# Deformable attention, local part: dense rows of all heads in one transfer per tile, A in one per head, values by quarters in DRAM, all on SP's queue

## The chip, the cores and the metric

The program runs on one core of a Trainium2 chip, in float32. The metric is the device time of one execution in microseconds. Before the change three runs took 7682.11, 7709.34 and 7716.46 us, with a median of 7709.34. One further execution was recorded by the hardware profiler; all durations of instructions come from it.

## What is computed

The network has four layers on x (4 images of 64 x 64 positions, 128 channels). The change is in the first operator of the first layer, a deformable attention with four heads of 32 channels. Everything after it is untouched. Cut to what matters:

```python
qkv = depthwise3x3(x @ w_qkv + b_qkv) + b_dw
mask = sigmoid(conv1x1(pconv(q)))                  # 9 taps, the same for all heads
for i in range(4):                                 # heads
    off = conv1x1(pconv_i(q))                      # (dy, dx) for each of 9 taps
    dil = 2 * i + 1                                # 1, 3, 5, 7
    k_i = bilinear(k[i], p + dil * tap + off) * mask
    v_i = bilinear(v[i], p + dil * tap + off) * mask
attn = softmax(q . k_i over the 9 taps);  out = (attn . v_i) @ w_proj + b_proj;  x = x + out
```

A bilinear sample at an offset of at most one pixel is a weighted sum over a 3 x 3 neighbourhood of the tap, with "hat" weights max(0, -o), 1 - |o|, max(0, o) in y and in x. The local part computes it so; a general branch exists for larger offsets and is not taken with these inputs.

## The kernel before, in words

**Stage.** `stage_deformable` (L366) runs `deformable_project` for the four images, then one of two branches. `deformable_project` (to L607) makes q, k, v and the offsets, and stores them in DRAM: qd and kd by channel, vd as 80 columns x 84 rows x 128 channels with a border of zeros, od (offsets and masks). Per image SP's queue carries, in order, the stores of q (L529), the reload of q (qc, L548) and its shifted copies (qs, L554), the stores of k, and od (L594). The stores of v (L571) are on ACT's queue.

**Local part.** `deformable_near` (L610) takes tiles T = 0..127, 32 for each image. A tile is two image rows, 128 positions, in units of 8 columns. Four tiles are a group c, for which DVE and POOL work at once. The stages of a tile and a group, by the main loop's step T (LAG = 14):

- `products` (L713): POOL copies the tile's queries into a block layout, two instructions at L721, into one of two tiles qm.
- `product` (L738): PE multiplies them with the padded keys kpad, 64 matmuls (L750), into four PSUM tiles S of one buffer each; `copy_products` copies them to band on ACT (L760).
- `hats` (group c at T = 4c): POOL turns the offsets of the group (tile of, loaded at L686) into hat weights (L694 to L702; mk at L700 holds the masks, and L702 multiplies them in). `hat_products` multiplies the hat weights in y and x to H, 3 x 3 weights for each tap (L708, one for each head, 324 elements). H has three buffers.
- `attention` (T = 4c + 4, L762): a unit's 128 positions lie on partitions, so each partition needs its own window of band. Copies under a mask shift the rows by the bits of the column (L771, by 4, 2, 1), and a first one (L768) by the bit of the image row. Then band times H (L775), a sum over 9 (L782), and a maximum (L790 to L792).
- `spread` (T = 4c + 7, L795): the exponential on ACT (L798), the sum and its reciprocal, and the weights times H into A, 9 instructions for heads 1 to 3 (L805), t0 for head 0 (L811), and its sum into A by 12 small ones (L815 to L818).
- `write` (T = 4c + 9, L820): A goes to DRAM, in dd, one tensor for each head and each of two buffers. It takes 16 DMAs: 4 heads x 4 quarters of 32 partitions, because the image row moves the start of a row by 3 elements. The contiguous pieces are 240 to 816 B.
- `read_dense` (T + 12, L833): dd is read back as dense rows for one tile, where the row step of dd makes each position's window land in its place. It takes 4 DMAs, one for each head, of 120 to 192 KB; heads 0 and 2 on SP's queue, 1 and 3 on ACT's (L837).
- `values` and `value_block` (T + 14, L842 and L855): v comes in blocks of 4 image rows, each as 4 DMAs of 256 KB, one for each quarter of the columns (L849), seven buffers.
- `transpose` (T + 14): 12 PE transposes of the dense rows (L868), 3 copies on ACT (L870). `weigh` multiplies them with the values (L888). After four tiles `values_done` copies the result (L900), loads x (xg, L904) and adds the bias on POOL (L905); `projection` multiplies by w_proj (L911), and POOL adds (L914); `store` writes (L920).

**What sets the order.** The instruction order of each engine and queue is fixed when the program is built. The scheduler of the framework moves work ahead where its tiles are free; `block` and `behind` (L674 to L680) put the steps' work behind PE's last block. A DMA is an instruction on SP's or ACT's sequencer. It waits for what it depends on there, and all behind it waits too. In steady state POOL's built order for four tiles, with n the group of the queries, is: qm of tile 4n, the sum L914, qm of 4n+1 and 4n+2, L905, mk, the four H products of a group (they wait for DVE's release of the buffer), qm of 4n+3, and the hats of the next group. ACT's order for a tile is: the three copies of the transposes, the tile's two D reads, in some tiles the exponential, then the four copies to band.

Of the kernel before, what the change touches and what calls it, by code (L numbers as in the profile page):

```python
# [10 lines left out]
F32 = mybir.dt.float32  # L11
I32 = mybir.dt.int32
AF = mybir.ActivationFunctionType
ALU = mybir.AluOpType
# [351 lines left out]
def stage_deformable(k, x, y, w_qkv, b_qkv, w_dw, b_dw, pconv, w_offT, b_off, grid, masks, w_proj, b_proj):  # L366
# [12 lines left out]
    nc, tc = k.nc, k.tc  # L379
    with ExitStack() as octx:  # L380
# [6 lines left out]
        far = deformable_project(k, fp, x, qd, kd, vd, od, w_qkv, b_qkv, w_dw, b_dw, pconv, w_offT, b_off)  # L387
        with tc.If(far > 0) as branch:
            deformable_general(k, x, y, w_qkv, b_qkv, w_dw, b_dw, pconv, w_offT, b_off, grid, w_proj, b_proj)
        with branch.Else():  # L390
            deformable_near(k, dr, x, y, qd, kd, vd, od, masks, w_proj, b_proj)


def deformable_project(k, fp, x, qd, kd, vd, od, w_qkv, b_qkv, w_dw, b_dw, pconv, w_offT, b_off):
# [7 lines left out]
    nc, tc = k.nc, k.tc  # L402
    HP = 66
    with ExitStack() as ctx:
# [129 lines left out]
        for b in range(4):  # L534
# [57 lines left out]
            for i in range(4):  # L592
                r, h = divmod(i, 2)
                nc.sync.dma_start(od[b][64 * h + 32 * r : 64 * h + 32 * r + 32], off[32 * i : 32 * i + 32])  # L594

# [13 lines left out]
def deformable_near(k, dr, x, y, qd, kd, vd, od, masks, w_proj, b_proj):  # L609
# [23 lines left out]
    PP = [12 * (15 + w) for w in W]  # L633
    with ExitStack() as ctx:
# [14 lines left out]
        for t in qms:  # L649
            nc.gpsimd.memset(t, 0.0)  # L650

# [5 lines left out]

        dd = [[dr.tile([128, 4 * PP[g] + 12], F32, tag=f"dd{i}{g}", name=f"dd{i}{g}") for g in range(4)] for i in range(2)]

        dense = [wp.tile([128, 4, 384], F32, tag=f"D{i}", name=f"D{i}") for i in range(4)]  # L660
        for t in dense:
            nc.gpsimd.memset(t, 0.0)
        for i in range(2):
            for g in range(4):
                zero = dense[g].rearrange("p t n -> p (t n)")
                eng = (nc.sync, nc.scalar)[g % 2]
                eng.dma_start(dd[i][g][:, 0 : 4 * PP[g]], zero[:, 0 : 4 * PP[g]])
                eng.dma_start(dd[i][g][:, 4 * PP[g] : 4 * PP[g] + 12], zero[:, 0:12])

        Hs, bands, outs, vblocks, logits, ofs, hat_of, queries = {}, {}, {}, {}, {}, {}, {}, {}  # L670
        accs, lefts, project, stores = {}, {}, [], []
# [16 lines left out]
        def hats(c):  # L688
# [10 lines left out]
            mk = sm.tile([128, 3, 4, 3], F32, tag="mk", name="mk")  # L699
            nc.gpsimd.tensor_copy(mk, window(of, 72, [[3, 3], [81, 4], [1, 3]]))  # L700
            hy = hat[:, 0:4].rearrange("p s a t n i -> p s (a t n) i")
            nc.gpsimd.tensor_tensor(hy, hy, window(mk, 0, [[0, 4], [1, 36], [0, 3]]), op=ALU.mult)  # L702
            Hs[c] = sm.tile([128, 4, 36, 9], F32, tag="H", name="H", bufs=3)

        def hat_products(c, groups):
            H, hat = Hs[c], hat_of[c]
            for g in groups:
                nc.gpsimd.tensor_tensor(  # L708
                    H[:, g].rearrange("p n (a c) -> p n a c", a=3), window(hat, 108 * g, [[3, 36], [1, 3], [0, 3]]),
                    window(hat, 108 * (4 + g), [[3, 36], [0, 3], [1, 3]]), op=ALU.mult,  # L710
                )
# [50 lines left out]
        def attention(c):  # L762
            H, band = Hs[c], bands.pop(c)
            prod = sm.tile([128, 4, 36, 9], F32, tag="prod", name="prod", bufs=1)
            for g in range(4):
                rows = lambda off, dims: window(band[g], off, [[4 * CW[g], 12]] + dims)
                n = 3 * CW[g]
                nc.vector.copy_predicated(rows(0, [[1, n]]), bit[:, 0, :, 3:4].to_broadcast([128, 12, n]), rows(CW[g], [[1, n]]))  # L768
                for i, s in enumerate((4, 2, 1)):
                    n = W[g] + s - 1  # L770
                    nc.vector.copy_predicated(  # L771
                        rows(0, [[CW[g], 3], [1, n]]), bit[:, :, :, i : i + 1].to_broadcast([128, 12, 3, n]), rows(s, [[CW[g], 3], [1, n]])
                    )
                for tx in range(3):
                    nc.vector.tensor_tensor(  # L775
                        window(prod, 324 * g + 9 * tx, [[27, 12], [3, 3], [1, 3]]),
                        window(band[g], DIL[g] * tx, [[4 * CW[g], 12], [CW[g], 3], [1, 3]]),
                        window(H, 324 * g + 9 * tx, [[27, 12], [3, 3], [1, 3]]), op=ALU.mult,
# [16 lines left out]
        def spread(c):  # L795
# [7 lines left out]
            for g in range(1, 4):  # L803
                for ty in range(3):
                    nc.vector.tensor_tensor(  # L805
                        window(A[g], ty, [[12 * DIL[g], 12], [3, 3], [12, 3]]), window(H, 324 * g + 108 * ty, [[9, 12], [3, 3], [1, 3]]),
                        window(lg, 36 * g + 12 * ty, [[1, 12], [0, 3], [0, 3]]), op=ALU.mult,
                    )

            t0 = sm.tile([128, 36, 9], F32, tag="t0", name="t0", bufs=1)  # L810
            nc.vector.tensor_tensor(t0, H[:, 0], window(lg, 0, [[1, 36], [0, 9]]), op=ALU.mult)  # L811
            for ty in range(3):
                a0 = lambda m0, n: window(A[0], 12 * m0 + ty, [[60, 4], [12, n], [3, 3]])
                tap = lambda tx, s0, n: window(t0, 108 * ty + 9 * tx + s0, [[27, 4], [1, n], [3, 3]])
# [5 lines left out]
        def write(c):  # L820
            A = As[c % 2]
            for g in (1, 2, 3, 0):
                d, P = dd[c % 2][g], PP[g]
                for j in range(4):
                    r = j % 2
                    nc.sync.dma_start(
                        bass.AP(
                            d.tensor, d.offset + 32 * j * (4 * P + 12) + 3 * r, [[4 * P + 12, 32], [P, 4], [1, 12 * W[g]]]
                        ),
# [1777 lines left out]
```

## Time and profile before

| What | Value |
|---|---|
| median of three runs | 7709.34 us (7682.11 to 7716.46) |
| the profiled execution | 7690.3 us; its span 7688.3 us |
| projection, 0 to 675 us | PE busy 566 us, DVE 126, ACT 209, POOL 11; DMA share 0.44, 105 GB/s |
| local part, 675 to 1830 us | PE busy 839 us, DVE 732, ACT 373, POOL 466; DMA share 0.71, 203 GB/s |
| granted TensorE clock | 0.94 in the first of these, 0.82 in the second |
| value blocks, vb<-vd | 272 DMAs of 256 KB |
| dense rows, D<-dd | 512 DMAs of 120 to 192 KB, half on SP, half on ACT |
| A, dd<-A | 512 DMAs of 30 to 102 KB for each head and group |

A line of the timeline has the start in us, the length, the engine, the line of the kernel, the operation, its output and inputs and their shapes; an "x4" merges four neighbours, and what stands in brackets is the engine's idle time before it and what ended it. SPq and ACTq are the DMA issues of these sequencers. A line of waits has who waited, for what, the total, the number of times and the longest. The granted clock is a share of full speed. A DMA share is the mean busy share of the 16 DMA engines.

### The profile page before, as it was taken

The page shows a single profiled execution, that of the slowest core. Times are in us where ns is not written, and L with a number is a line of the kernel's source. Part 1 is how long each engine was busy: PE and PEld are TensorE (multiplying, and loading weights), DVE is VectorE, ACT ScalarE, POOL GpSimd, SP SyncE. Part 2 cuts the span into 40 slices and gives each one's busy share as a digit, 9 for nine tenths or more (in the row PEclk, how much of TensorE's full clock was granted, in tenths as well). Part 3 has the DMA queues.
Part 4 walks back from the last instruction along what each step waited for, and adds up shares of the span by engine and source line. Part 5 has one row for each costly group of instructions (what it writes and reads, how often), then busy time and mean ns, then how long its engine had stood idle before and what let it go on. Part 6 is the DMA issues. An engine that isn't in the chain of part 4 may idle for free. (4 is left out here: it accounts for less than half of the span.)

```text
span 7688.3 us, 157708 instructions
## 1 busy us (share of the span) xinstructions
PE 6522.7 (85%) x63791; PEld 3542.4 (46%) x63791; DVE 4821.5 (63%) x11178; ACT 2690.3 (35%) x6141; POOL 1741.4 (23%) x1634
## 2 busy tenths in 40 slices
PE   7995777775688868989989999798898997997989
PEld 3343666663455644345555555445225234242244
DVE  2113766764277554858856656674785875867877
ACT  3331333333234313611146555565104013031056
POOL 0003444320001100035532221154012112120135
PEclk9997887887799889999999988798897997988989
DMA  4436677775400022030100000001111111111101
GB/s 121 98 87 179 187 209 205 213 199 172 143 4 1 2 60 48 10 117 22 27 12 10 9 10 6 9 1 30 39 25 49 26 33 40 25 35 38 25 23 31
DMA packets 678781, 495.59 MB, mean 64 GB/s; under 512 B 302326, under 2 KB 594104, under 8 KB 674200
## 3 DMA queue, kind: packets, MB, share of 16 engines
q1 hardware_dynamic: 480910, 354.59, 17.0%
q10 hardware_dynamic: 197130, 130.77, 6.2%
q8 instruction: 509, 8.34, 0.5%
q14 instruction: 232, 1.90, 0.1%
HBM read 335.28 MB, written 149.75 MB: 63 GB/s over the span
## 5 line engine op out<-in xcount | busy, mean ns | idle before, releaser
L2476 DVE TENSOR_TENSOR t<-S,q 128x1536 f32<-128x1536 f32 (+3 forms) x608 | 1156.9, 1948 | 123.2 <-PE S L2464 117.9
L2464 PE MATMUL S<-R,L 32*128 32x512 f32 x4096 | 734.6, 651 | 90.3 <-DMA R<-wd 78.9
L2492 PE MATMUL acc<-t,sum 128*32 128x512 f32 x4096 | 639.5, 608 | 0.0
L750 PE MATMUL S<-kpad,qm 32*64 32x240 f32 (+3 forms) x8192 | 403.4, 421 | 216.0 <-ACT band L760 97.5
L2178 PE MATMUL pe<-ew,yT 128*128 128x512 f32 x1024 | 479.4, 603 | 27.4 <-DVE xs L2184 24.5
L1777 PE MATMUL acc<-w,attT 128*64 128x264 f32 x4096 | 486.3, 391 | 10.4 <-DVE w L1773 10.4
L2464 PEld LDWEIGHTS S<-R,L 32*128 32x128 f32 x4096 | 200.6, 186 | 611.4 <-issue 280.4
L2498 ACT COPY agg<-acc 128x512 f32<-128x512 f32 x32 | 18.8, 586 | 1194.0 <-DMA L<-pd 626.7
L750 PEld LDWEIGHTS S<-kpad,qm 32*64 32x64 f32 x8192 | 299.9, 156 | 271.5 <-issue 136.9
L1770 POOL TENSOR_TENSOR w<-xtl,ei 128x528 f32<-128x528 f32 x256 | 332.1, 1319 | 309.6 <-ACT ei L1769 204.5
L2184 DVE SCALAR_TENSOR_TENSOR xs<-pe,gate,xs 128x128 f32<-128x128 f32 x1024 | 332.5, 345 | 96.5 <-PE pe L2178 79.8
L1773 DVE TENSOR_TENSOR w<-xtl,pe 128x1056 f32<-128x1056 f32 x256 | 320.3, 1251 | 100.3 <-ACT ei L1769 89.4
L1777 PEld LDWEIGHTS acc<-w,attT 128*64 128x64 f32 x4096 | 284.0, 137 | 197.5 <-DVE w L1774 38.0
L2187 ACT ACTIVATE sc<-pe,gate 128x128 f32<-128x128 f32 x1024 | 291.3, 374 | 202.2 <-PE pe L2178 194.1
L514 PE MATMUL dw<-pad,diag 32*32 32x512 f32 x6912 | 310.4, 614 | 12.9 <-issue 7.0
L2507 POOL TENSOR_TENSOR o<-o,bf 128x512 f32<-128x512 f32 x32 | 40.7, 1271 | 1229.4 <-ACT o L2506 1229.4
L760 ACT COPY band<-S 128x144 f32<-128x144 f32 (+3 forms) x512 | 136.0, 351 | 480.4 <-DMA D<-dd 152.3
L2492 PEld LDWEIGHTS acc<-t,sum 128*32 128x32 f32 x4096 | 92.7, 108 | 458.4 <-issue 436.1
L2178 PEld LDWEIGHTS pe<-ew,yT 128*128 128x128 f32 x1024 | 185.6, 193 | 234.3 <-issue 151.4
L768 DVE COPY_PREDICATED band<-bit,band 128x432 f32<-128x432 int32 (+3 forms) x128 | 107.5, 895 | 270.0 <-ACT band L760 264.2
L868 PE MATMUL pt<-ident,D 128*128 128x128 f32 x1536 | 243.0, 315 | 29.2 <-DMA D<-dd 15.2
L771 DVE COPY_PREDICATED band<-bit,band 128x288 f32<-128x288 int32 (+11 forms) x384 | 243.0, 742 | 0.0
(520 smaller groups left out, 13065.8 us busy)
## 6 DMA issues: line engine op xcount, KB each, us to landing
vb<-vd SPq DMA_DIRECT2D x272, 256.0 KB
D<-dd ACTq DMA_DIRECT2D x128, 192.0 KB
D<-dd SPq DMA_DIRECT2D x128, 168.0 KB
D<-dd ACTq DMA_DIRECT2D x128, 144.0 KB
w<-in_e_weight_dram ACTq DMA_DIRECT2D x16, 1024.0 KB
w<-in_e_weight_dram SPq DMA_DIRECT2D x16, 1024.0 KB
wd<-s SPq DMA_DIRECT2D x32, 512.0 KB
D<-dd SPq DMA_DIRECT2D x128, 120.0 KB
```

The lines of the kernel that those rows point to most:

```text
L514: nc.tensor.matmul(acc[g][32 * c : 32 * c + 32], diag[r, j, tap, :], pads[j][r, y0 : y0 + 8, tx : tx + 64], start=(tap == 0), stop=(tap == 8),
L750: ins = nc.tensor.matmul(acc[g][64 * h : 64 * h + 64].rearrange("p (a s) c -> p a s c", a=3), qm[rows, h, m, :], keys, start=(m == 0), sto ...
L771: nc.vector.copy_predicated(rows(0, [[CW[g], 3], [1, n]]), bit[:, :, :, i : i + 1].to_broadcast([128, 12, 3, n]), rows(s, [[CW[g], 3], [1, ...
L1770: nc.gpsimd.tensor_tensor(w2[:, 2:4], xt[:, 2:4, 0:2], window(ei, 0, [[0, 2], [0, 2], [1, 132]]), op=ALU.mult)
L1773: nc.vector.tensor_tensor(w1, xt[:, :, 1:3], window(pe, 0, [[0, 4], [0, 2], [1, 132]]), op=ALU.mult)
L1777: nc.tensor.matmul(acc[b // 2][64 * (b % 2) : 64 * (b % 2) + 64], attT[:, b // 2, hp, 64 * (b % 2) : 64 * (b % 2) + 64], src[:, b].rearran ...
L2178: nc.tensor.matmul(pe[h].rearrange("p e c -> p (e c)"), yT[:, 128 * t : 128 * t + 128], ew[:, 4 * h : 4 * h + 4, :].rearrange("p e c -> p ...
L2184: nc.vector.scalar_tensor_tensor(xt, pe[0][:, e, :], gate[:, t, e : e + 1], xt, op0=ALU.mult, op1=ALU.add)
L2187: nc.scalar.activation(sc[:, e, j, :], pe[1][:, e, :], AF.Copy, scale=gate[:, t, 4 + e : 5 + e])
L2464: nc.tensor.matmul(S[:, j, :], Ls[n % 2][r, ag, :], Rs[n % 2][r, ag].rearrange("p x y -> p (x y)"), start=True, stop=True)
L2476: nc.vector.tensor_tensor(t[:, j0:j1].rearrange("p u (x y) -> p u x y", x=8), S[:, j0:j1].rearrange("p u (x y) -> p u x y", x=8), qf[:, q0 ...
L2492: nc.tensor.matmul(acc[0][32 * h : 32 * h + 32, :], sum4, t[:, j, :], start=(u < 4), stop=(u >= 60))
```

## The change

It has six parts. In the projection, each image's padded values are copied from vd to a new tensor vq in DRAM, four overlapping quarters of 32 columns side by side, by four DMAs on SP's queue. In the local part a value block is then one DMA of 1 MB with 8 KB rows. The dense rows of all heads lie in one tensor dd for each buffer, 384 elements a head, and come in one DMA a tile (768 KB, 6 KB rows) on SP's queue, zeros with them. A goes out in one DMA a head. For that the shift by the image row moves out of the address and out of band into the weights: H has 4 x 3 weights for each tap where it had 3 x 3, and `hats` builds the four y weights from the three, the masks and the row bit; L768 goes, the shifts of band and the products with H and A cover a fourth row, and the quarters of `write` go. H has two buffers where it had three, dt three for four. xg is loaded at the first tile of its group, four tiles before. The zeros for dd come from one tile, in ten DMAs on ACT's queue. ACT issues no D reads any more.

In the built program the steady order on POOL for four tiles is: qm of 4n, mk and the sum L914, the row-bit products of mk, L905, qm of 4n+1 and 4n+2, two H products, half of the qm of 4n+3, a third H product, the other half, the fourth, and the hats of the next group. On SP's queue, one of an image's four copies to vq stands ahead of od, and three behind it.

```diff
+        vq = [dr.tile([32, 84, 4, 128], F32, tag=f"vq{b}", name=f"vq{b}") for b in range(4)]
...
             for i in range(4):
                 r, h = divmod(i, 2)
                 nc.sync.dma_start(od[b][64 * h + 32 * r : 64 * h + 32 * r + 32], off[32 * i : 32 * i + 32])
+            for q in range(4):
+                nc.sync.dma_start(vq[b][:, :, q, :], vd[b][16 * q : 16 * q + 32])
...
+    ROW = 4 * 4 * 384 + 12
+        nc.vector.tensor_copy(row, bit[:, 0, 0, 3:4])
-        dd = [[dr.tile([128, 4 * PP[g] + 12], F32, tag=f"dd{i}{g}", name=f"dd{i}{g}") for g in range(4)] for i in range(2)]
+        dd = [dr.tile([128, ROW], F32, tag=f"dd{i}", name=f"dd{i}") for i in range(2)]
-        for t in dense:
-            nc.gpsimd.memset(t, 0.0)
...
+        nc.gpsimd.memset(dense[0], 0.0)
+        zero = dense[0].rearrange("p g n -> p (g n)")
+        for d in dd:
+            for t in range(4):
+                nc.scalar.dma_start(d[:, 1536 * t : 1536 * t + 1536], zero)
+            nc.scalar.dma_start(d[:, 6144:ROW], zero[:, 0:12])
...
-            nc.gpsimd.tensor_copy(mk, window(of, 72, [[3, 3], [81, 4], [1, 3]]))
+            nc.gpsimd.tensor_copy(mk[:, 0].rearrange("p (a t n) -> p a t n", a=3, t=4), window(of, 72, [[3, 3], [81, 4], [1, 3]]))
+            nc.gpsimd.tensor_scalar(mk[:, 1], mk[:, 0], row, None, op0=ALU.mult)
+            nc.gpsimd.tensor_tensor(mk[:, 0], mk[:, 0], mk[:, 1], op=ALU.subtract)
             hy = hat[:, 0:4].rearrange("p s a t n i -> p s (a t n) i")
-            nc.gpsimd.tensor_tensor(hy, hy, window(mk, 0, [[0, 4], [1, 36], [0, 3]]), op=ALU.mult)
-            Hs[c] = sm.tile([128, 4, 36, 9], F32, tag="H", name="H", bufs=3)
+            h4 = hy_of[c] = sm.tile([128, 4, 36, 4], F32, tag="hy", name="hy", bufs=1)
+            nc.gpsimd.tensor_tensor(h4[:, :, :, 0:3], hy, at(0), op=ALU.mult)
+            nc.gpsimd.tensor_tensor(hy, hy, at(1), op=ALU.mult)
+            nc.gpsimd.tensor_tensor(h4[:, :, :, 1:3], h4[:, :, :, 1:3], hy[:, :, :, 0:2], op=ALU.add)
+            nc.gpsimd.tensor_copy(h4[:, :, :, 3], hy[:, :, :, 2])
+            Hs[c] = sm.tile([128, 4, 36, 12], F32, tag="H", name="H")
...
-                nc.vector.copy_predicated(rows(0, [[1, n]]), bit[:, 0, :, 3:4].to_broadcast([128, 12, n]), rows(CW[g], [[1, n]]))
                 for i, s in enumerate((4, 2, 1)):
                     n = W[g] + s - 1
-                    nc.vector.copy_predicated(
-                        rows(0, [[CW[g], 3], [1, n]]), bit[:, :, :, i : i + 1].to_broadcast([128, 12, 3, n]), rows(s, [[CW[g], 3], [1, n]])
-                    )
+                    nc.vector.copy_predicated(flat[:, :, 0:n], bit[:, 0, :, i : i + 1].to_broadcast([128, 48, n]), flat[:, :, s : s + n])
...
         def write(c):
-            for g in (1, 2, 3, 0):
-                d, P = dd[c % 2][g], PP[g]
-                for j in range(4):
-                    r = j % 2
...
+            for g, d in enumerate(DIL):
+                m = dd[c % 2]
+                nc.sync.dma_start(
+                    bass.AP(m.tensor, m.offset + 384 * g + 12 * (7 - d), [[ROW, 128], [1536, 4], [1, 12 * W[g]]]),
+                    As[c % 2][g][:, :, 0 : W[g]].rearrange("p t c s a -> p t (c s a)"),
+                )
         def read_dense(T):
             c, t = divmod(T, 4)
-            for g, d in enumerate(DIL):
-                m, P = dd[c % 2][g], PP[g]
-                (nc.sync, nc.scalar)[g % 2].dma_start(
...
+            m = dd[c % 2]
+            nc.sync.dma_start(
+                dense[t].rearrange("p g n -> p (g n)"), bass.AP(m.tensor, m.offset + 1536 * t, [[16 * ROW, 8], [ROW - 12, 16], [1, 1536]])
+            )
         def value_block(n):
-            for q in range(4):
-                nc.sync.dma_start(
-                    t[:, q].rearrange("p s c -> p (s c)"),
-                    bass.AP(d.tensor, d.offset + 16 * q * 10752 + 4 * kb * 128, [[10752, 32], [128, 4], [1, 512]]),
-                )
+            nc.sync.dma_start(
+                t.rearrange("p s q c -> p (s q c)"), bass.AP(d.tensor, d.offset + 4 * kb * 512, [[84 * 512, 32], [512, 4], [1, 2048]])
+            )
         def values(T):
             if T % 4 == 0:
+                inputs[0] = sm.tile([128, 4, 128], F32, tag="xg", name="xg")
+                nc.sync.dma_start(inputs[0], tokens(x, b, i, 4))
...
-                dt = sm.tile([128, 4, 128], F32, tag="dt", name="dt", bufs=4)
+                dt = sm.tile([128, 4, 128], F32, tag="dt", name="dt", bufs=3)
...
-                xg = sm.tile([128, 4, 128], F32, tag="xg", name="xg")
-                nc.sync.dma_start(xg, tokens(x, b, 4 * c, 4))
+                xg = inputs[0]
```

The products with H and A in `attention` and `spread` change their shapes from 3 x 3 to 4 x 3 and are not shown.

## The prediction

> **What bounds the kernel now.** Only the deformable stage is edited. In the table of stretches it fills the first 1830 of 7688.3 us: the projection to about 667 us, the local part from 671 to 1830. I first looked at three groups of four tiles in the middle of the local part (columns: the stretch and its length, busy PE, weight loads, DVE, ACT, POOL with instruction counts, the granted clock, the DMA share, GB/s):
>
> ```profile
> core 0: us, PE busy (x) PEld busy (x) DVE busy (x) ACT busy (x) POOL busy (x), PEclk, DMA share, GB/s
> 1412.85:1445.93 33.08, 24.18 (x694) 20.39 (x695) 23.07 (x58) 11.43 (x32) 12.05 (x20) 0.91 0.74 209
> 1445.93:1479.39 33.46, 24.34 (x700) 20.29 (x698) 23.20 (x57) 11.42 (x32) 12.42 (x20) 0.94 0.77 217
> ```
>
> No engine is full: a group takes 33 us, PE and DVE work 23 to 24 of them, the DMA engines three quarters. So a chain of waits sets the period. The view of waits over 660 to 1830 us names its links (who waited for what: total us, times, longest):
>
> ```profile
> POOL xg L905 <- DMA xg<-in_x_dram: 411.1, 24, 24.8
> ...
> ACT band L760 <- DMA D<-dd: 152.3, 29, 8.3
> ...
> PE S L750 <- ACT band L760: 97.5, 48, 6.1
> PE S L750 <- POOL qm L721: 94.0, 22, 16.6
> DVE m L799 <- ACT lg L798: 90.0, 32, 6.8
> ...
> ACT lg L798 <- DMA D<-dd: 82.6, 11, 9.4
> ```
>
> ACT, only a third busy, is held up by its own queue: it issues two of a tile's four reads of dd (L837), and while such an issue waits, the copies and the exponential behind it wait too. The timeline of one group shows where that hurts:
>
> ```profile
> 1427.44 0.31 DVE L792 TENSOR_TENSOR lg<-lg,me 128x144 f32<-128x144 f32 x1
> 1428.35 0.32 ACT L798 ACTIVATE lg<-lg 128x144 f32<-128x144 f32 x1 [6.19 <-DMA D<-dd]
> ...
> 1433.20 3.15 POOL L708 TENSOR_TENSOR H<-hat 128x324 f32<-128x324 f32 x4 [1.59 <-DVE t L811]
> ...
> 1436.30 0.45 POOL L721 COPY qm<-q 128x64 f32<-128x64 f32 x2
> ...
> 1437.55 2.20 PE L750 MATMUL S<-kpad,qm 32*64 32x144 f32 x64
> ...
> 1444.35 1.22 ACTq L837 DMA_DIRECT2D D<-dd  x2
> 1445.61 1.07 ACT L760 COPY band<-S 128x144 f32<-128x144 f32 x4 [7.24 <-DMA D<-dd]
> 1445.93 1.33 DVE L768 COPY_PREDICATED band<-bit,band 128x432 f32<-128x432 int32 x2 [8.74 <-ACT band L760]
> ```
>
> This is a closed loop, once per group. DVE's attention (1445.93 to 1460.92, 15.0 us) ends in the exponential on ACT; DVE's spread reads H until L811 (done at 1433.12); then POOL may overwrite an H buffer (L708); behind that in POOL's order stands the query copy qm; it releases PE's product of the group's last tile; its copy (L760) lets the next attention start. The product ended at 1439.75 and its copy began at 1445.61: 5.9 us behind a DMA issue. SP's own rows in these three groups (1412.85 to 1514.23) sum to 79.8 of 101.4 us of issuing: 16 writes, 8 reads and about 8 value transfers a group, each some 0.4 to 0.65 us and more beside ACT's. That is why the rows that ACT waits for land late. The exponential starts at 732.8 the first time and 1772.0 the last, so 31 periods of 33.5 us.
>
> **The change in the loop, per group.** Working against one period:
>
> - DMA issues. Reads of dd fall from 16 to 4, writes from 16 to 4, value transfers from about 8.5 to 2.1; q, x, store, offsets and keys (about 5.5) stay. SP goes from about 38 issues to 16; even at 0.7 us that is 11 us where 26 stand now. ACT issues none. The 5.9 us ahead of the copy become its usual 0.1; of the exponential's wait (90.0/32 = 2.8 us) about 0.4 stays, as at 758.74, where nothing stood in front.
> - DVE attention. The row select goes (L768: 107.5 us / 32 = 3.4). The three shifts cover 48 rows, not 36: L771 is 243.0 / 32 = 7.6 now; its rows run in steps of four elements (5, 6 and 8 wide take 527, 480 and 502 ns; 9, 10, 12 take 665, 676, 655), so about 1 ns an element on a third more, +1.9. L775 goes from 108 to 144 elements, 12 x 0.038 = +0.45; L782 from 1296 to 1728, +0.45. Net -0.5: 14.5 us.
> - DVE spread, from L799 to the end of L811: 4.4 now, +0.35 for nine products a third larger, +0.1 for L811; L805 took 2.92 us in this group because POOL's L905 ran beside it, 1.93 at 784.68 where none did, and L905 moves away. I take 4.5.
> - POOL. H grows from 324 to 432 elements. L702 does 432 in 1.0 us, so a product costs 1.05 for 0.79. In the changed order three of the four, not four, precede the whole qm copy: 3.2 + 0.45 = 3.65, for 3.6 now. H has two buffers for three, so POOL makes H one group less ahead; in both orders the qm of a group's last tile stands behind the same spread, so this adds no link.
> - PE's product with its start 3.3 (2.2 to 2.9 by clock) and the first copy 0.35.
>
> Sum: 14.5 + 0.8 (exponential with its handoffs) + 4.5 + 3.65 + 3.3 + 0.35 = 27.1 us.
>
> **What the loop then collides with.** Behind H, POOL does the next hats: today 1.4 + 1.15 + 0.7 + 0.6 + 1.0 (L694 to L702), now also a second 432 product, a 288 sum and a 144 copy: 7.0 us, ahead of the query copy of the next tile. From one qm to the next that is 8.6 us, then three unhindered steps of PE (5.0 us from 1201.96 to 1206.98) and a projection of 2: 25.9. PE alone needs 4 x 5.1 + 2 = 22.5, DVE 23.1 as now. The DMA engines: 7.67 MB a group (D is 768 KB a tile for 624, writes 1.08 MB, values 2.2 MB, the rest 1.0). At the near rows' 282 GB/s (the ACT queue moved 5.65 MB between 1100 and 1240 in 14.3% of 16 x 140 us) 27 us, at the 380 of the weight loads' rows of about 2 KB (2070 to 2080) 20. D and values, 5.4 MB in rows of 6 and 8 KB, are nearer to the second, the rest stays at 250: 23.5. All four limits stand within 5 us of the loop.
>
> The attention will also start while POOL is still in its hats, which today end before it (hats to 1441.66, attention from 1445.93). Row: at 706.96, with POOL full, the attention took 21.2 us to L792 for 15.0, so +0.4 us for each us beside POOL; against nothing, if the overlap misses the sharing instructions. About 5 us overlap, +1.7 (0 to 4). I take the period as 27.1 + 1.7 = 28.8. **Gain: 31 x (33.5 - 28.8) = 146 us.**
>
> On this point the Trainium skill speaks against the change: "SBUF — State Buffer", section "Who interferes with whom", says a DVE instruction with two SBUF inputs and a GpSimd instruction that reads SBUF share a port pair, and the second blocks entirely. By that rule the whole 5 us would be lost, a period of about 32 and a gain near 45 us; the row of 706.96 shows a partial loss only, and decides here.
>
> The skill's "DMA: Bandwidth & Descriptors", section "Issuing engines are not separate DMA queues", says that several issuing engines save only the time of issue, usually small. By it the ACT queue's end would be worth 8 x 0.6 = 4.8 us a group at most; the trace shows an issue that waits, 5.9 us on one copy alone, and that is what the sum counts.
>
> **What it costs outside the loop.** The new copies vd to vq: 16 transfers, 2688 pieces of 512 B each (1.38 MB). No row moves DRAM to DRAM. At least one read, by the 512 B rows of the x reload (290 GB/s from 1840 to 1860): 4.7 us; at most read and write in turn, the write by the ACT queue between 50 and 600 us (9.44 MB in 7.0% of 16 x 550 us, 245 GB/s): 10.4. So 19 to 42 us a batch, 14 to 31 for the three behind od. From od to the next store of q there are 49, 49 and 29 us (224.5 to 273.5, 378.2 to 427.1, 531.5 to 560.1): hidden, and if not, it adds to PE's wait for qc (22.6 us in 4). I take +3. After the last batch the cover is gone: od ends at 663.6, the first keys are issued at 678.1, and PE waits 19.5 us for them. Keys and queries stand behind three copies in SP's queue: 678 to 695, so +0 to +25; one memset of dense for four (5.3 us) gives POOL some back, but ten zero issues on ACT come before its first copies. I take +12. At the drain, PE waits 9.4 us for D at 1790; half of it goes: -5.
>
> **Sum:** 7690.3 (span 7688.3 and 2.0 around it) - 146 + 12 + 3 - 5 = 7554. The median of the runs is 7709.3, 19 us above that execution; less the same 136 it is 7573. I say 7560.
>
> **Rivals.**
> 1. The sharing costs nothing and the loop settles at 26.5 (PE and DVE's work with handoffs). For: L816's 0.77 beside H falls after L811, off the loop. Against: 7 us of hats. 31 x 7 - 12 = 205 less: 7485. Chance 0.17.
> 2. DVE and POOL block each other in attention and hats, or the one queue runs full: period 31.3. For: 706.96, and 85% of DMA time on one queue. 31 x 2.2 - 25 = 43 less: 7650. Chance 0.12.
> 3. Slower: the vq copies. One ring takes SP's transfers in turn; if a batch's copies last D us, the delays over four batches are about 4D less the gaps 49 + 49 + 29 + 15 = 142. That equals the gain in the loop, 146, at D = 72 us, 77 GB/s, beyond my upper bound by a factor 1.7; at D = 85 the time is 7690 - 146 - 5 + 198 = 7737. For: no row of such a copy; against: 512 B rows in both directions run above 240 GB/s. Chance 0.07.
> 4. The change does not remove the wait: SP in order holds read_dense behind write, write waits for the spread, and the transposes wait for D in place of ACT. Against: the next read needs no row of that write and has two steps, some 13 us, to land. Period 33: 7700. Chance 0.04.
>
> My forecast has 0.60, between 7500 and 7630. The range takes in most of rivals 1 and 2: 7470 to 7670. A change under 0.5% (38 us) cannot be told from none here: faster 0.86, same 0.06, slower 0.08.
>
> **What would show it.** No ACT issue of D, and the wait of the band copies for D gone; the exponential 0.4 us after L792; POOL's 411 us for xg gone; attention near 15 us but 1 to 3 longer where hats run beside it; exponentials 28 to 29 us apart; the first product of the local part at 685 to 710. Wrong if the attention reaches 18 us, if PE waits for D, or if the projection grows by more than 10 us.

## The result, and the profile after

The changed kernel takes 8144.1 us (median of 4 runs, 8142.0 to 8167.6), the kernel before 7696.8 us beside it (4 runs): a ratio of 1.059, 95% interval 1.055 to 1.062. The forecast was 7560 us, faster. The profiled execution has a span of 8142.0 us for 7688.3, 453.7 us more. In the local part the first exponential comes at 762.7 us (732.8 before) and the last at 2212.1 (1772.0). So 31 periods of 46.75 us stand where there were 31 of 33.5, which makes 410 us; 30 us come ahead of the first exponential, 14 behind the last. The period went the wrong way.

First the two groups of the changed kernel that answer to those shown of before (same columns: stretch and length, busy PE, weight loads, DVE, ACT, POOL, clock, DMA share, GB/s):

```profile
1414.81:1466.65 51.84, 29.21 (x860) 25.36 (x858) 20.33 (x53) 14.40 (x35) 15.32 (x25) 0.73 0.74 152
1466.65:1514.60 47.95, 20.70 (x626) 17.05 (x620) 21.43 (x53) 10.47 (x28) 12.49 (x21) 0.68 0.69 149
```

The engines do about as much work in a group as before (PE 49.9 us in these two groups for 48.5, DVE 41.8 for 46.3), the rest of the time they stand. The DMA share is the same 0.7, but it moves 150 GB/s where it moved 209 to 217. The granted clock is lower too (0.73 and 0.68 for 0.91 and 0.94), but that is not the loss: the product that stands in the loop took 2.2 us in both kernels in the median (table below). The view of waits, 760 to 2260 us, all engines and then SP's own:

```profile
DVE band L782 <- ACT band L773: 701.7, 28, 37.9
...
PE S L763 <- POOL qm L734: 487.2, 36, 30.1
POOL mk L707 <- DMA of<-od: 438.9, 21, 24.5
POOL xg L906 <- DMA xg<-in_x_dram: 435.1, 29, 33.8
```

```profile
SPq L832 <- DMA D<-dd: 495.8, 35, 22.8
SPq L921 <- POOL mk L708: 207.8, 12, 18.7
SPq L921 <- POOL xg L915: 172.4, 13, 19.9
```

ACT's waits for D are gone, as forecast. In their place POOL waits for two small loads (offsets of, and x), 28 us a group together; PE waits for POOL's query copies, DVE for PE's products. One group in the timeline shows how it goes round:

```profile
1414.81 2.39 SPq L832 DMA_DIRECT2D dd<-A  x4
...
1418.59 0.59 SPq L840 DMA_DIRECT2D D<-dd  x1
...
1420.09 1.00 SPq L691 DMA_DIRECT2D of<-od  x1
...
1438.20 0.22 POOL L707 COPY mk<-of 128x36 f32<-128x36 f32 x1 [24.51 <-DMA of<-od]
...
1438.38 1.26 POOL L915 TENSOR_TENSOR xg<-xg,o 128x512 f32<-128x512 f32 x1
...
1439.67 0.37 SPq L921 DMA_DIRECT2D x<-xg  x1
...
1441.96 0.38 SPq L862 DMA_DIRECT2D xg<-in_x_dram  x1
...
1451.16 1.26 POOL L906 TENSOR_TENSOR xg<-xg,bpj 128x512 f32<-128x512 f32 x1 [10.66 <-DMA xg<-in_x_dram]
1452.36 0.76 POOL L734 COPY qm<-q 128x64 f32<-128x64 f32 x4
...
1452.65 4.11 PE L763 MATMUL S<-kpad,qm 32*64 32x144 f32 x64 [14.91 <-POOL qm L734]
```

The offsets are issued at 1420.09 and POOL has them at 1438.20, 18 us later: in the same queue stand writes, a dense read and a value block. Meanwhile SP stands in the store (1439.67), which waits for POOL's addition (1438.38), which stands behind mk. So xg is issued only at 1441.96, POOL waits for that too, and the queries come last. PE's product, after 14.9 us of standing, takes 4.11 us here for the usual 2.2.

The links of the loop, from the starts and ends of these instructions, as medians over the 7th to 28th group (us; the rows are the prediction's; the experiments e10 to e17 are told below):

```
                                 before  after   e1    e10   e12*   e11*  e17*
exponential to last read of H      4.8    4.4    4.4   4.5    4.4    4.5   4.5
from there to H written (POOL)     3.3   17.3    7.8   3.8    3.2    4.2   3.8
to the product's start             2.8    7.1    8.0   6.0    1.4    4.1   0.8
product                            2.2    2.2    2.3   2.2    2.2    2.2   2.2
its end to DVE's attention         3.4    0.4    0.4   0.4    2.5    0.4   0.5
attention, to the exponential     17.3   17.0   16.4  16.4   17.0   17.6  19.1
period, mean of all 31            33.5   46.8   39.5  33.9   30.3   32.9  30.6
(* dense reads cut short; a median of each row need not add up to the mean)
```

The prediction's gain is there in one row, 3.4 to 0.4. Two rows, POOL's H and the way from it to the product, take 18 us back.

**The DMA engines.** A packet is one contiguous piece of a transfer, as the profile records it. From the records of single packets, 1200 to 1600 us (own sums over all sizes that occur more than 60 times, by the trace's own clock, 11 us ahead of that of the views):

```
                             before   after     e1      e8
a write of 816 B, ns           50      121      92      52
256 B loads, ns                19       32      20      21
D packets, B: ns         960 to 1536:  6144:   6144:   6144:
                          53 to 79      387     430     416
all packets, us of 400 x 16   4643     4577    5352    4999
```

In the kernel before, ACT's queue carries nothing but dense reads there, and each transfer leaves small completion packets of 4 B: 736 with the 11776 rows of 92 reads (by the clock of the views), 8.0 for each. The source of a dense read has 8 in its outermost dimension, 16 x 8 rows in all. Read as one completion packet for each engine that takes part, a dense read lay on 8 of the 16 engines; the changed kernel's has the same 8 outermost, and e3 below counts 8.0 for it too. The mean share hides that. Of the changed kernel's 4577 us, 1583 are dense packets: 1583/8 + 2994/16 = 385 of 400 us on these 8, 96%. For the kernel before the same sum gives 1606/8 + 3037/16 = 391 of 400, 98%. The records don't name the engine of a packet, so these two sums take the other packets as even over all 16.

The Trainium skill, "DMA: Bandwidth & Descriptors", section "Rules for kernel authors", states this: an outermost dimension of fewer than 16 confines a transfer to at most that many engines. The 8.0 packets agree; the page was not weighed in the prediction.

### The profile page after: what moved, and what is told of

Same layout as the page of the kernel before. It is cut to its first block, busy times and chain, and to the rows that moved or that the text cites. A ratio compares the mean times of both kernels' runs of the same rounds, so it can differ in the third digit from the quotient of the medians.

```text
span 8142.0 us, 156307 instructions
## 1 busy us (share of the span) xinstructions
PE 6531.4 (80%) x63791; PEld 3555.1 (44%) x63791; DVE 4781.7 (59%) x11051; ACT 2707.9 (33%) x6141; POOL 1798.3 (22%) x1791
## 5 line engine op out<-in xcount | busy, mean ns | idle before, releaser
L763 PE MATMUL S<-kpad,qm 32*64 32x288 f32 (+3 forms) x8192 | 388.1, 432 | 600.8 <-POOL qm L734 504.6
L782 DVE COPY_PREDICATED band<-bit,band 128x384 f32<-128x384 int32 (+11 forms) x384 | 318.1, 938 | 752.6 <-ACT band L773 701.7
L872 ACT COPY dt<-pt 128x512 f32<-128x512 f32 x384 | 209.6, 592 | 307.9 <-PE pt L870 306.0
L870 PE MATMUL pt<-ident,D 128*128 128x128 f32 x1536 | 263.8, 335 | 36.9 <-issue 21.0
```

Of the source, the lines that this page charges most:

```text
L763: ins = nc.tensor.matmul(acc[g][64 * h : 64 * h + 64].rearrange("p (a s) c -> p a s c", a=3), qm[rows, h, m, :], keys, start=(m == 0), sto ...
L782: nc.vector.copy_predicated(flat[:, :, 0:n], bit[:, 0, :, i : i + 1].to_broadcast([128, 48, n]), flat[:, :, s : s + n])
```

## Experiments

Three theories stood at the start. **A**: the 8 engines that carry the dense reads set the period. **B**: the one queue on SP does, through what stands behind what. **C**: the layout of values, with its copies and its large packets. D, E and F were formed on the way. Times are medians; those of the kernel before lay between 7682 and 7693 us beside them.

**e1: the changed kernel, dense reads over 16 engines.**

```diff
-bass.AP(m.tensor, m.offset + 1536 * t, [[16 * ROW, 8], [ROW - 12, 16], [1, 1536]])
+bass.AP(m.tensor, m.offset + 1536 * t, [[ROW - 12, 16], [16 * ROW, 8], [1, 1536]])
...
-nc.scalar.copy(dt, pt)
+nc.scalar.copy(dt.rearrange("p g (b x) -> p g b x", b=8), pt.rearrange("p g (x b) -> p g b x", b=8))
```

> The changed kernel, with the 128 rows of a dense read taken in another order: the outermost dimension of the source has 16 steps in place of 8, and the copy of the transposed tile puts the order back. Bytes, packets, queue and number of transfers stay. Theory A (a dense read lies on 8 of the 16 DMA engines; these 8 are 96% busy in the changed kernel and set the period of a group at 47.5 us): with 16 engines the sum of all packets, 2268 us in a stretch of 200 us, is 539 us a group and 34 us on each engine, less where packets get shorter with fewer in flight; period 28 to 35 us, time 7550 to 7730 us. Theory B (one queue on SP: writes of dd wait for reads of D, and everything behind them is late): a read lands some 2 us earlier, period 44 to 47 us, time 8030 to 8140 us. Theory C (packets of 6 and 8 KB move fewer bytes in a us than those of 1 and 2 KB): period 40 to 47 us, time 7900 to 8140 us.

7920.4 us, 39.5 us a group. The stretch from 1200 to 1600 us, of the changed kernel and then of e1:

```profile
1200.00:1600.00 400.00, 204.40 (x5489) 171.26 (x5473) 164.94 (x424) 97.46 (x248) 120.26 (x195) 0.71 0.71 153
```

```profile
1200.00:1600.00 400.00, 263.39 (x6726) 219.21 (x6718) 224.89 (x513) 120.65 (x304) 164.88 (x247) 0.75 0.84 187
```

A is right in kind: 7.2 of the 13.2 us a group go, and the share rises from 0.71 to 0.84. It isn't all; 39.5 lies outside its range. The time alone would also lie in C's range; e4 tests C.

**e2: the kernel before, the same order in its four reads.**

```diff
-bass.AP(m.tensor, m.offset + t * P, [[16 * (4 * P + 12), 8], [4 * P, 16], [1, P]])
+bass.AP(m.tensor, m.offset + t * P, [[4 * P, 16], [16 * (4 * P + 12), 8], [1, P]])
```

> The kernel before, with the same order of 16 in its four dense reads a tile and in the copy. Theory A: the low 8 engines were 98% busy there too (566 us of dense packets over 8 engines and 1073 us of others over 16 make 138 of 140 us), so the period of 33.5 us was theirs; with 1639 us over 16 engines (102 of 140 us) the next limit takes over at 27 to 31 us, time 7490 to 7620 us. Rival (the prediction's loop of engines with ACT's issues in it sets 33.5 us whatever the DMA engines do): 7660 to 7720 us.

7653.4 us, ratio 0.9955 (0.9938 to 0.9971), 32.2 us a group, 16.0 completion packets a read for 8.0. Between the two: the 8 engines cost the kernel before 1.3 us a group. Its 98% was not a bound: with half of the dense load taken off these 8 only 4% of the period went. Spread over 16, packets of 1536 B took 86 ns for 79, so a packet's time holds waiting too, and such sums overstate the work.

**e3: the changed kernel, dense reads of odd tiles on ACT.**

```diff
-nc.sync.dma_start(
+(nc.sync, nc.scalar)[T % 2].dma_start(
```

> The changed kernel with the dense reads of odd tiles issued by ACT, those of even tiles by SP. Theory A: every read still lies on the same 8 engines; period 46 to 48 us, time 8090 to 8180 us. Theory B (the one queue): half of the reads no longer stand ahead of SP's writes and loads; period 34 to 42 us, time 7700 to 7980 us.

8035.4 us, 42.4 us a group, between both ranges, with 8.0 completion packets a read: 4.3 us a group come from the second queue alone, with 8 engines as before. So the 96% of the changed kernel was no bound either. The run does not part what stands behind a large read in the queue from what SP, in order, issues late.

**e4: the changed kernel with the value blocks of before** (from vd, four transfers; no copies to vq).

> The changed kernel with the value blocks of before: no copies to vq, four transfers a block, packets of 2 KB. Theory A: the same bytes lie on all 16 engines; packets of 2 KB took 107 ns before, 4 of them 428 ns, against 591 ns of one of 8 KB in the changed kernel, so 2 blocks a group cost up to 2.6 us less on each engine, and the copies of the start (15 us) go: period 44 to 47.5 us, time 8010 to 8130 us. Theory C (the large value packets or the copies are the loss): period 33 to 38 us, time 7690 to 7850 us.

8100.4 us, 45.8 us a group, and the first exponential 9.5 us earlier: as A had it. C is worth 1.0 us a group.

**e5: e1 with three buffers of dd** (`range(3)`, `c % 3`).

> Run e1 (changed kernel, reads of D over 16 engines: 39.5 us a group, 7920 us) with three buffers of dd in memory in place of two, so that a write of dd no longer waits for reads of two groups earlier (305.8 us of SP's waits in e1, 9.5 us a group). Theory B (SP's one queue stands still behind that wait, and all its other loads come late): period 31 to 35 us, 7680 to 7800 us. Theory A, as e1 left it (the work of the DMA engines: sum of all packets 33.4 us a group on each of 16 engines, 85% of the time; what waits in SP's queue would only wait in the engines): period 37 to 39.5 us, 7850 to 7930 us.

7891.6 us, 38.35. The wait of SP's writes for D left the list; in its place the writes waited 250 us for DVE's A (44.5 in e1), and SP's store waited 370 us for POOL, as long as in e1 (366 us). B in this form falls: the queue stands as before, behind other waits.

**e6: e1 with e3's edit.**

> Run e1 with the reads of D of odd tiles issued by ACT. In the changed kernel itself the same edit took 109 us off (46.75 to 42.4 us a group). Theory B: SP is relieved of half of the large reads, period 33 to 36 us, 7720 to 7810 us. Theory A as e1 left it: the engines' 33.4 us a group stay, period 37 to 39.5 us, 7850 to 7930 us.

7806.8 us, 36.15, the time at the upper end of B's range, the period just above it: a second queue is worth 3.4 us a group on 16 engines too.

**e7: e1 with four dense reads a tile, of the used columns only.**

```diff
+for g, d in enumerate(DIL):
+    o, n = 12 * (7 - d), 12 * (15 + W[g])
+    nc.sync.dma_start(
+        dense[t][:, g, o : o + n],
+        bass.AP(m.tensor, m.offset + 1536 * t + 384 * g + o, [[ROW - 12, 16], [16 * ROW, 8], [1, n]]),
+    )
```

> Run e1 with each dense read in four, one a head, of the columns that the head uses (as in the kernel before: 624 KB a tile for 768, packets of 960 to 1536 B for 6144), all on SP. Theory A as e1 left it (bytes and packet times): a tile's 128 rows cost 128 x (0.053 + 0.069 + 0.068 + 0.079) = 34 us of engine time by the packets of before in place of 128 x 0.43 = 55 us, 5.2 us a group on each engine; period 33 to 36 us, 7720 to 7830 us. Theory B (waits in SP's queue): SP issues 12 more transfers a group and still waits; period 38 to 42 us, 7880 to 8010 us.

7847.9 us, 37.8, neither range: 1.8 us a group for 19% fewer dense bytes, a third of the 5.2 that A had. Packets of 960 and 1536 B took 80 and 102 ns here, not the 53 and 79 of before.

**e8: e1 with rows of dd 512 B longer** (`ROW = 4 * 4 * 384 + 12 + 128`).

> Run e1 with rows of dd 512 B longer, so that the rows that 16 engines read at once lie 25088 B apart and not 24576 B (6 x 4096). Theory D (rows at multiples of 4 KB hit the same part of the memory, so that a packet of 6144 B takes 430 ns in e1 for 234 ns where one read runs alone): packets of 300 ns or less, 4 us a group less on each engine, period 34 to 36 us, 7750 to 7830 us. Theories A and B: no change, 39 to 40 us, 7900 to 7940 us.

7857.6 us, 37.4. The time fits neither range. The theory had the wrong object: the dense packets hardly changed (430 to 416 ns), but the writes of 816 B fell from 92 to 52 ns, the time of before, and the value packets of 8 KB from 525 to 420. That the longer rows do this is measured; which of the two the 2.1 us a group come from, and why, is not known. The writes have a row step of 24624 B and the reads one of 24576, and the edit lengthens both.

**e9: e1 with all dense reads on ACT.**

> Run e1 with all reads of D issued by ACT, so that SP's queue holds no large read. Theory B (small loads and writes of SP land late because they stand behind D in one queue): beyond e6 (half of the reads on ACT: 36.15 us a group, 7807 us) a further gain, 33 to 35.5 us, 7700 to 7790 us. Theory A (16 engines' work, 84 to 87% busy in e1 and e6): 36 to 37 us, 7800 to 7840 us. Rival (ACT's copies wait behind its issues, as in the kernel before): 37 to 41 us, 7840 to 7960 us.

7855.0 us, 37.7, worse than half of them on ACT. The time lies in the rival's range, but ACT's waits show no D among the larger ones, so the rival isn't shown. SP's waits don't explain it either: its store waited 355.2 us for POOL's addition (101.1 in e6), but the load of xg behind it waited less for the store to land, 99.1 us for 324.2, and so did the writes for D, 231.7 us for 339.8. Why e9 is slower than e6 stays open.

**e10: all that helped, together** (e6, e8's rows, e5's buffers, e4's values).

> All that helped, together: the changed kernel with reads of D over 16 engines, odd tiles' reads on ACT, rows of dd 512 B longer, three buffers of dd, and the value blocks of before without the copies to vq. If the parts add up (from e6's 36.15 us a group: the stride 2.1 by e8, the third buffer 1.2 by e5, the values 1.0 and 10 us at the start by e4): 31.9 us a group, 7630 to 7720 us. If they share one wait: 33.5 to 35.5 us, 7720 to 7790 us.

7728.6 us, ratio 1.0041 (1.0027 to 1.0054), 33.9 us: the parts do not add up to 31.9; time and period lie in the range of parts that share one wait. 416 of the 447 us are back, and the changed kernel is still not the faster one.

**e11: the changed kernel with dense reads of 96 columns for 1536** (three more memsets at the start).

> The changed kernel with dense reads cut to 96 of 1536 columns (the output lacks the rest of the local attention); every instruction, wait and transfer stays, only the bytes of D go. Prediction's loop of engines (28.8 us, and 28 to 30 us between the first exponentials of the changed kernel, before any dense read): 28 to 30.5 us a group, 7560 to 7640 us. Theory B in its strong form (order in SP's queue and not bytes): 36 us or more, over 7800 us.

7690.1 us, 32.9, neither. The bytes of D cost 13.8 of 46.75 us. What stays is 4.1 us over the 28.8 of the prediction's loop. Two of e11's waits, from 760 to 1850 us:

```profile
PE S L764 <- POOL qm L735: 193.7, 46, 10.7
...
POOL H L722 <- DVE t L821: 166.7, 28, 11.9
```

**e12: the kernel before with dense reads of 24 columns a head.**

> The kernel before with its four dense reads a tile cut to 24 columns each (the output lacks the rest of the local attention); all instructions and waits stay. If its loop of engines is the one seen between its first exponentials, before any dense read (24.6 to 25.5 us): 25 to 28 us a group, 7430 to 7530 us: then the change made the loop 4 us longer and the kernel before was held back by its reads. If ACT's waiting issues set 33.5 us as the prediction had it, whatever the bytes: 31 to 33.5 us, 7610 to 7700 us.

7589.2 us, 30.3, neither. Here D's bytes cost 3.3 us. So **without the bytes the change makes the loop 2.7 us longer** (30.3 to 32.9), where the prediction had it 4.7 us shorter. The two waits of e11 are 31.8 and 53.5 us here. The second, POOL's wait for an H buffer, points at a rival that no run tries: H with two buffers for three (and dt with three for four).

**e13, e14, e15: offsets two steps earlier, the store one step later** (in e11, in e10, and in e2, there with xg loaded early as well).

```diff
-step(T, -2, offsets, 4)
+step(T, -4, offsets, 4)
...
-late = list(stores)
+late = [s for s in stores if T >= s[3] + 2]
```

> Run e11 (changed kernel, reads of D cut to 96 columns: 32.9 us a group, 7690 us) with the load of the offsets two tile steps earlier and the store of the result one step later (the output still lacks the rest of the local attention). In e11 SP stands 301.6 us (10 us a group) in the store behind POOL's addition of the result, POOL then stands behind the load of the offsets that SP issues later. Theory E (SP and POOL, each in order, wait for each other in turn, and this makes 32.9 of the 28.8 that the prediction had): 29 to 31 us, 7570 to 7640 us. Rival F (POOL's own work, 19 us a group for 14 in the kernel before, and its stretches beside DVE): 32 to 33.5 us, 7660 to 7710 us.

> Run e10 (changed kernel with 16 engines, two queues, wider rows, a third dd, values as before: 33.9 us a group, 7729 us) with the same two moves. Theory E: 30.5 to 32.5 us, 7620 to 7690 us. Rival F or the DMA engines (88% busy in e10): 33 to 34.5 us, 7700 to 7740 us.

> Run e2 (kernel before with reads of D over 16 engines: 32.2 us a group, 7653 us) with the same two moves and with xg loaded at the first tile of its group, as in the changed kernel. POOL's waits for xg (278.8 us and 124.7 us, 12 us a group in e2) go. If they are on the path: 29 to 31 us, 7530 to 7610 us; if not: 32 to 33 us, 7630 to 7680 us.

7687.7, 7726.4 and 7651.1 us: no change from e11, e10 and e2. That is as rival F had it, but it does not refute E, because the moves did not take the waits away. From the first exponential to the last, SP's store waited 280.9 us for POOL's addition in e13 (282.6 in e11) and 145.8 in e14 (128.0 in e10), and POOL waited 408.9 us ahead of adding to xg in e15 (371.1 in e2). So E stays open, and in the changed kernel itself it wasn't tried.

**e16: e14 with the query copies on ACT.**

```diff
-nc.gpsimd.tensor_copy(
+nc.scalar.copy(
     window(qm, 256 * h, [[32, 2], [72, 4], [1, 8]]),
```

> Run e14 with the copies of the queries (qm) on ACT in place of POOL. In e11 a copy of 36 elements on POOL that began in DVE's attention took 5.28 us in place of 0.3, in the kernel before a qm copy up to 8.8 us in place of 0.24, and the products wait for qm. Theory F (POOL is held up beside DVE and its order carries qm): 1.5 to 3 us a group less than e14, 50 to 90 us. Rival (ACT, in order, then brings qm behind its copies of products): same as e14 or up to 60 us slower.

7707.2 us (7698.3 to 7729.5), some 19 us less than e14 (7712.6 to 7749.4). That is a smaller gain than F's and not the rival's loss; the DMA share is 0.90, so another limit may stand near.

**e17: the same edit in e11. e18: in e2.**

> Run e11 (changed kernel with reads of D cut to 96 columns, output without the rest of the local attention) with the copies of the queries on ACT: e16 made the same edit where the DMA engines were 90% busy, here they are at 53%. In e11 a POOL copy that began at 1389.36 in DVE's attention lasted 5.28 us, to 0.06 us after the attention's last product, and the query copies behind it came at 1396.63. Theory F (POOL and DVE hold each other up in the attention, and POOL's order carries the queries): the product no longer waits for POOL, 29 to 31.5 us a group, 7580 to 7650 us. Rival (the loop of DVE's attention, POOL's H and three steps of PE is the limit itself): 32 to 33 us, 7665 to 7700 us.

> Run e2 (kernel before with reads of D over 16 engines, 32.2 us a group, 7653 us) with the copies of the queries on ACT. There a query copy on POOL that began in the attention lasted up to 8 us, and POOL's waits for xg stood ahead of others. Theory F: 30 to 31.5 us, 7580 to 7630 us, faster than both kernels. Rival (ACT's own issues of D stand ahead of the copies): 32 to 34 us, 7650 to 7710 us.

e17: 7611.3 us, 30.6 us a group, 79 us less than e11, in F's range, and PE's wait for the queries, 193.7 us in e11, left the list. e18: 7619.6 us, 31.6 a group; **ratio 0.9909 (0.9892 to 0.9926), faster than both kernels**. So it is shown that the queries' place in POOL's order cost 2.3 us a group in e11 and 0.6 in e2. What makes POOL late ahead of them is not shown by these edits: its work, its waits and its being held up beside DVE all stood there. In e18 POOL's waits ahead of adding to xg even grew, from 371 to 585 us, and the kernel got faster: a wait costs by what stands behind it. The holding up is seen in e11's timeline (L708 there is L707 of the changed kernel):

```profile
1387.13 6.16 DVE L783 COPY_PREDICATED band<-bit,band 128x768 f32<-128x768 int32 x6
1389.36 5.28 POOL L708 COPY mk<-of 128x36 f32<-128x36 f32 x1 [5.67 <-DMA of<-od]
1393.14 1.43 DVE L785 TENSOR_TENSOR prod<-band,H 128x144 f32<-128x144 f32 x6
...
1396.63 0.93 POOL L735 COPY qm<-q 128x64 f32<-128x64 f32 x4
1396.92 1.72 PE L764 MATMUL S<-kpad,qm 32*64 32x144 f32 x27 [6.03 <-POOL qm L735]
```

A copy of 36 elements, else 0.2 to 0.3 us long, began in the attention and ended with DVE's last product: 1389.36 + 5.28 = 1394.64, and 1393.14 + 1.43 = 1394.57. The queries wait behind it, and PE for them. Such a long one is rare in e11: two copies of mk between 740 and 1690 us. The kernel before had eight of its query copies lasting 3.8 to 8.8 us there, each ending within 0.1 us of the end of a DVE instruction, as at 1310.75:

```profile
1310.75 8.98 POOL L721 COPY qm<-q 128x64 f32<-128x64 f32 x2 [2.37 <-PE S L750]
...
1318.30 1.17 DVE L775 TENSOR_TENSOR prod<-band,H 128x108 f32<-128x108 f32 x6
```

The Trainium skill, "SBUF — State Buffer", section "Who interferes with whom", calls the pair of ports that DVE and GpSimd share an exclusive lock, where the later one blocks fully. These rows agree that POOL, coming later, stood still: DVE's six copies took 6.16 us beside it, and 6.18 at 1424.68 in the changed kernel with POOL idle. But the page has the lock held for one instruction, and here POOL stood through the rest of six copies and through six products. DVE lost time as well: its attention lasted 17.4 us in e11 and 19.0 in e17, 15.1 in the changed kernel, where POOL mostly stands waiting.

## Why the prediction was wrong, point by point

- **ACT's issues in the loop: right.** The 5.9 us ahead of a copy became 0.1 in the group shown; in the median of the groups the row fell from 3.4 to 0.4, so the gain in this row was 3 us and not nearly 6. The group shown was among the worse ones.
- **"The DMA engines: ... 23.5": the step that failed.** In the 400 us stand the packets of 8 groups (4096 writes of 816 B, 512 a group), so the transfers of a group took 4577/8/16 = 35.8 us of each engine, had all 16 shared them. The bytes ran at 7.67 MB in 35.8 us, 214 GB/s, and not at the 326 that 23.5 needs: rows of 6 and 8 KB were taken to be like the weight loads, but reached 16 and 15 GB/s an engine. And the sum divided by 16 what for the dense reads lay on 8. So the prediction had the DMA engines below its loop, at no cost; with the bytes of D all but gone, 13.8 of the 46.75 us went (e11). Taken in this order, the 8 engines account for 7.2 us (e1), a second queue for a further 3.4 (e6), row step, third buffer and values for 2.3 more together (e10).
- **"Behind H, POOL does the next hats": mis-sized by the unseen load.** The step counted POOL's instructions (3.65 us with qm) but not that mk waits for of, and xg for x, both behind D in the one queue: 17.3 us. In e10 the row is 3.8. The sign "POOL's 411 us for xg gone" failed with it: 435.1 us, though xg is issued four tiles before.
- **The sharing of DVE and POOL, "+1.7 (0 to 4)": too small.** The attention took 14.5 in the sum; with POOL mostly waiting it was 15.1 (the changed kernel), with POOL beside it 16.4 (e10), 17.4 (e11) and 19.0 (e17). The prediction's other reading, that the whole overlap is lost and the period about 32, came nearer: 32.9 (e11). And the loss on the other side, a POOL instruction held to the attention's end with the queries behind it, was not in the sum. Between the first exponentials the periods were 28.1 to 29.8 us, just the loop of the forecast, with an attention of 18.6 to 18.9, past the 18 us that the prediction named as a sign of being wrong. The kernel before ran 24.6 to 25.5 there. That could be read beforehand, and set beside the sum of 28.8 it says that the loop grows. The expectations of e11 and e12 put these periods before any dense read; that is not so, the first were issued at 776.2 and 738.4, but only a few had run.
- **Costs outside: too low.** The start cost 30 us for 12. PE's first product came at 705.9 for 685.2, inside the range given, and ACT's first copies at 721.8 for 695.0, behind the ten issues of zeros. The copies to vq made up 9.5 us of it (e4). Behind the last exponential 14 us were lost, where the drain was to gain 5. The projection grew by 3.4 us (od issued at 663.6 for 660.2), as forecast.
- **Rivals.** The second ("the one queue runs full: 31.3") named half of the mechanism with the wrong price; it took the mean share too. The fourth (SP holds reads behind writes) was half right, and its transposes were not the ones that waited. No rival asked how many engines a transfer uses.

What stays open: what makes the loop without the bytes 2.7 us longer (DVE beside POOL, POOL's larger work ahead of the queries, the H buffers), why large dense packets take 390 to 430 ns, why the writes are slow with these row steps and fast with both 512 B longer, why all reads on ACT (e9) are worse than half of them (e6), and what holds e10 at 33.9 us with the engines 88% busy.

## What to carry to other kernels

Count the completion packets of a transfer, or look at the outermost dimension of its access pattern, before you divide its bytes by 16: a mean DMA share of 0.7 can be 8 engines that are busy nearly all the time. Move the reads before you believe such a sum: it holds waiting, and here 96% was no bound. Merging transfers saves issues but puts everything in one order; look for the small load that then stands behind the large ones, and at the in-order engine that waits for it. An instruction on POOL next to DVE's two-input work can last as long as that work: ask what stands behind it, and whether another engine could do it.

## What was not expected of the hardware

- Larger dense packets ran slower: 1536 B at 19.4 GB/s an engine in the kernel before, 6144 B at 15.9 in the changed kernel and 14.3 over 16 engines (e1). It is not the size alone: value packets of 8192 B ran at 14.6 in the changed kernel and 20.4 in e6.
- Writes of 816 B took 50 ns in the kernel before, 121 in the changed one, 92 in e1, and 52 with rows 512 B longer (e8).
- Copies of 64 elements on POOL lasted 0.24 us, or up to 8.8 us when they began in DVE's attention, to the end of a run of DVE instructions.
